# Graph 0's receiver logits on VectorE and the last graph's first row on TensorE, in a four-layer graph-network kernel on one core

## The chip, the cores and the metric

The kernel runs on one core of a Trainium2 chip. The metric is the device time of one execution in microseconds (us). Three runs of the kernel before took 2438.94, 2440.05 and 2445.26 us, so the median is 2440.05. An execution with a profile took 2434.94 us; what the profile shows of it is a span of 2433.1 us.

A matrix product in float32 appears in the trace as two records, each with a weight load of its own. A transpose appears as one.

## The reference, cut to what matters

There are 16 graphs of 1024 nodes with 256 features, and a dense integer adjacency for each. Four layers follow one another; each begins with a layer norm and a ReLU and ends with a residual sum.

```python
# layer 0: attention, softmax over axis 1
h = jnp.matmul(input, W)
f1 = jnp.einsum('bnf,f->bn', h, a1)          # the receiver's logit
f2 = jnp.einsum('bnf,f->bn', h, a2)
e = leaky_relu(f1[:, :, None] + f2[:, None, :], 0.2)
attention = softmax(jnp.where(adj > 0, e, NEG_BIG), axis=1)
out = elu(attention @ h)
# layer 1: the same with softmax over axis -1
# layer 2: mean of the neighbours' messages, plus an update product and a bias, relu
# layer 3: four heads of 64; attention with slope 0.01, then per head:
out = relu(attention @ h + bias) + h
out = (out - mu) / sqrt(var + 1e-6) * ln_gamma + ln_beta
x = x + out
```

## The kernel before

The graphs are the outer loop. Each graph is a generator, `graph(b)` (L1272), that yields between small steps; the loop at L1319 pulls the generators in the order of due times, so that neighbouring graphs overlap. That order only fixes how the instructions are emitted. At the end `Order(tc, slots).run()` (L1348) lists them anew: it has a price for each instruction and a rank from TensorE's cumulative cost, walks through a model of the engines, and then fixes the order of each engine's queue. Each queue is served strictly in that order, so an instruction that waits holds all behind it.

A layer works on eight tiles of 128 nodes (NT = 8). `Norm.pair` (L854) takes two tiles: statistics, then `shifted` (L896) makes hn, the shifted and rectified tile, on ScalarE; `flip` (L904) transposes it on TensorE and ScalarE copies it into ht. The scale 1/std is not applied there, but at the eviction of the projection: `project` (L916) multiplies ht by the weights wx, to which one or two columns W a are appended, and an eviction on ScalarE (L999, L1061, L1172) multiplies by rs. rs comes from GpSimd (`inv_std`, L822), by a power.

The attention weight is not computed as exp(leaky_relu(f1 + f2)) but from products of exponentials: a tile of p (128 x 1024) is the larger of two terms times the mask (layer 0: L1027 and L1029; layer 1: L1088; layer 3: L1195). For that the receiver's logit must stand as a row on all partitions. There are two ways to get this row:

- `spread` (L925) and `everywhere` (L942): the column is transposed, its exponential is written to memory by a DMA (d_row), and a second DMA spreads it to all partitions (row). All layers with a row use it, apart from the next case.
- the class `Row` (L947): for each tile VectorE multiplies the identity by the logits (diag, L956), and TensorE multiplies a matrix of ones by diag (L957); two PSUM banks hold the row, and ScalarE writes its exponential (L963). Graph 0 uses it in layers 0 and 1.

In layer 0 the logit is column D of the evicted projection hs, so that each diag follows an eviction:

```python
            ps = project(norm, wx[0], n, D + 2)
            nc.scalar.activation(hs[:, n, : D + 2], ps[:, : D + 2], AF.Copy, scale=norm.rs[n])
            if by_pe:
                by_pe.add(n, hs[:, n, D : D + 1])
            m.step()
```

The mask is loaded in 16 raw pieces of 128 x 512 integers through SP's queue into three buffers (`Mask`, L779); `step` (L800) turns a piece into bytes and a sum, on VectorE for graph 0 (L808), on ScalarE for the others (L810), and starts the next load. After each p of layer 0, hs is divided by the sum of p (L1030, L1031), and the products with it go to PSUM. A part of the output tiles ("early", L1014 to L1016) is accumulated while the p's are still being made: four for graph 0, two for the others. The other tiles follow after the last p. For layer 0 each tile then has two evictions on ScalarE (L1049, L1051) and the residual on VectorE (`residual`, L979), which feeds the next norm.

PSUM has eight banks in four pools of two: tr (transposes), mm (projections and the prepared weight columns ps_wa), at and hd (output tiles; hd also for the row of the class `Row`, layer 2's outputs and layer 3's heads).

Some loads must not start too early: `behind` (L713) lets VectorE write one element of the target, copied from the latest p of graph 0, so that the load waits for that p.

In layer 3 (L1164) the four heads take eight p's each from a row per head; the row buffers are two. `tail` (L1220) then normalises each head: reciprocal and product, sum with hs, mean, squares on ScalarE (L1242), sums (L1250), the power on GpSimd, gamma, the scale (L1262), beta (L1264), the residual (L1268) and the output's DMA on SP (L1269). The tail of one graph lies beside the next graph's layers, except for the last graph's.

At the very end a count of conditions is taken (L1329 to L1347, t_bad and bad): were all values in range. It is summed over the partitions by TensorE (L1344) into a flag, which every engine reads (L1359); a general kernel runs if it isn't zero.

## Time and profile before

| What | Value |
|---|---|
| runs | 2438.94, 2440.05, 2445.26 us; median 2440.05 |
| profiled execution | 2434.94 us, span 2433.1 us, mean granted clock 0.991 |
| busy: TensorE, VectorE, ScalarE, GpSimd | 2355.2, 1966.0, 1448.6, 467.2 us |
| graph 0: first p (L1027) begins, last L1029 ends | 29.83, 49.99 us |
| graph 0: first product with a p (L1019) begins | 34.74 us |
| graph 0: first hs of layer 1 (L1061), first product of layer 1 (L1081) | 71.22, 83.34 us |
| last graph: layer 2's products end, first p of layer 3 | 2342.7, 2362.06 us |
| last graph: last p ends, last L1268 begins | 2400.4, 2425.20 us |

A line of the profile's groups or timelines names the line of the kernel, the engine, the operation, the tiles written and read, and the count; times are in microseconds after the start of the span. What stands in brackets is the time that the engine stood idle before and what ended that wait. The chain of waits goes back from the last instruction to what released each step.

### The profile page before, as it was taken

The page shows a single profiled execution, that of the slowest core. Times are in us where ns is not written, and L with a number is a line of the kernel's source. Part 1 is how long each engine was busy: PE and PEld are TensorE (multiplying, and loading weights), DVE is VectorE, ACT ScalarE, POOL GpSimd, SP SyncE. Part 2 cuts the span into 40 slices and gives each one's busy share as a digit, 9 for nine tenths or more (in the row PEclk, how much of TensorE's full clock was granted, in tenths as well). Part 3 has the DMA queues.
Part 4 walks back from the last instruction along what each step waited for, and adds up shares of the span by engine and source line. Part 5 has one row for each costly group of instructions (what it writes and reads, how often), then busy time and mean ns, then how long its engine had stood idle before and what let it go on. Part 6 is the DMA issues. An engine that isn't in the chain of part 4 may idle for free.

```text
span 2433.1 us, 63096 instructions
## 1 busy us (share of the span) xinstructions
PE 2355.2 (97%) x26224; PEld 2102.6 (86%) x26224; DVE 1966.0 (81%) x3862; ACT 1448.6 (60%) x4036; POOL 467.2 (19%) x454
## 2 busy tenths in 40 slices
PE   6999999999999999999999999999999999999974
PEld 5889888988988889888988989888888988989874
DVE  7478697997979889797896979889687897968858
ACT  4665657567475665756567475665757567475440
POOL 1020210303113031220303113031220303112021
PEclk9999999999999999999999999999999999999997
DMA  5452342624344253332624334253342624243031
GB/s 179 86 109 86 73 97 80 143 89 91 94 108 97 84 126 100 77 97 77 142 92 92 93 105 101 84 126 94 82 97 77 142 93 92 93 101 87 19 71 38
DMA packets 212152, 232.17 MB, mean 95 GB/s; under 512 B 10344, under 2 KB 160976, under 8 KB 211856
## 3 DMA queue, kind: packets, MB, share of 16 engines
q0 software_dynamic: 137728, 83.90, 19.2%
q1 hardware_dynamic: 74128, 144.14, 18.3%
q8 instruction: 208, 3.41, 0.6%
q14 instruction: 88, 0.72, 0.1%
HBM read 210.78 MB, written 17.22 MB: 94 GB/s over the span
## 4 chain that ended last, share of the span: by engine, by line
PE 87%; DMA 5%; ACT 3%; DVE 2%; issue 1%; POOL 1%; SPq 0%; POOLq 0%; ACTq 0%; DVEq 0%
PE ps_o L1019 18%; PE ps_o L1208 17%; PE ps_proj L919 17%; PE ps_o L1081 16%; PE ps_o L1149 10%; PE ps_o L1143 5%; DMA raw<-in_adj_t 4%; PE pt_h L913 4%; ACT mask L810 1%; POOL rs L826 0%; DMA d_row<-e_row 0%; ACT hn L900 0%; ACT hi L1135 0%; DMA row<-d_row 0%; DVE p L1088 0%
## 5 line engine op out<-in xcount | busy, mean ns | idle before, releaser
L1195 DVE SCALAR_TENSOR_TENSOR p<-row,q,mask 128x1024 f32<-128x1024 f32 x512 | 617.9, 1280 | 66.7 <-PE ps_o L1208 58.9
L919 PE MATMUL ps_proj<-wx,ht 128*128 128x258 f32 (+2 forms) x2048 | 512.8, 386 | 7.7 <-ACT hs L1172 3.9
L1208 PEld LDWEIGHTS ps_o<-hb,p 128*64 128x64 f32 x16384 | 488.5, 138 | 32.7 <-issue 17.8
L1208 PE MATMUL ps_o<-hb,p 128*64 128x65 f32 x16384 | 502.7, 223 | 9.5 <-DVE p L1195 7.6
L1019 PE MATMUL ps_o<-hs,p 128*128 128x256 f32 x2048 | 477.8, 381 | 8.7 <-ACT hs L1031 8.7
L1081 PE MATMUL ps_o<-hs,p 128*128 128x257 f32 x2048 | 469.0, 382 | 4.1 <-ACT v L1106 2.6
L1081 PEld LDWEIGHTS ps_o<-hs,p 128*128 128x128 f32 x2048 | 381.6, 190 | 61.8 <-ACT v L1106 6.2
L1019 PEld LDWEIGHTS ps_o<-hs,p 128*128 128x128 f32 x2048 | 380.2, 191 | 60.1 <-ACT hs L1031 10.1
L919 PEld LDWEIGHTS ps_proj<-wx,ht 128*128 128x128 f32 x2048 | 371.0, 190 | 68.6 <-ACT hs L999 6.1
L825 POOL TENSOR_SCALAR rs<-mv 128x4 f32<-128x4 f32 (+1 forms) x112 | 44.9, 401 | 1323.6 <-ACT unread L873 1307.2
L826 POOL TENSOR_TENSOR rs<-rs,neg_half 128x4 f32<-128x4 f32 (+2 forms) x144 | 264.0, 1833 | 12.0
L900 ACT ACTIVATE hn<-xs,shift 128x256 f32<-128x256 f32 x384 | 177.2, 503 | 79.8 <-PE pt_h L913 44.9
L1216 ACT ACTIVATE res<-ps_o 128x260 f32<-128x260 f32 x128 | 49.8, 389 | 259.8 <-PE ps_o L1208 259.3
L1149 PE MATMUL ps_o<-hi,adj 128*128 128x258 f32 x1024 | 202.1, 319 | 2.1 <-ACT hi L1135 1.0
L810 ACT ACTIVATE mask<-raw 128x512 uint8<-128x512 int32 x240 | 151.2, 633 | 50.2 <-DMA raw<-in_adj_t 49.5
L913 PE MATMUL pt_h<-ident,hn 128*128 128x128 f32 x1024 | 175.5, 278 | 4.6 <-ACT hn L900 4.3
L989 DVE SCALAR_TENSOR_TENSOR xs<-v,xs 128x256 f32<-128x256 f32 x384 | 160.7, 419 | 17.4 <-ACT v L1106 11.2
L818 POOL DMA_DIRECT2D adj<-in_adj x128 | 114.5, 898 | 293.7 <-PE ps_o L1149 292.0
L1149 PEld LDWEIGHTS ps_o<-hi,adj 128*128 128x128 f32 x1024 | 150.0, 190 | 14.9 <-ACT hi L1135 5.4
L1027 DVE SCALAR_TENSOR_TENSOR p<-row,q 128x1024 f32<-128x1024 f32 x128 | 161.5, 1272 | 1.7 <-DMA row<-d_row 1.4
L913 PEld LDWEIGHTS pt_h<-ident,hn 128*128 128x128 f32 x1024 | 126.7, 141 | 37.1 <-ACT hn L900 7.2
L1088 DVE SCALAR_TENSOR_TENSOR p<-row,q,mask 128x1024 f32<-128x1024 f32 x128 | 155.9, 1273 | 1.4 <-DMA row<-d_row 1.4
(115 smaller groups left out, 2988.1 us busy)
## 6 DMA issues: line engine op xcount, KB each, us to landing
raw<-in_adj_t SPq DMA_DIRECT2D x256, 256.0 KB
adj<-in_adj POOLq DMA_DIRECT2D x128, 512.0 KB, 5.2
row<-d_row SPq DMA_DIRECT2D x109, 512.0 KB
xs<-in_x POOLq DMA_DIRECT2D x32, 512.0 KB, 4.4
out<-xs SPq DMA_DIRECT2D x32, 512.0 KB
wx<-in_w SPq DMA_DIRECT2D x3, 256.0 KB
d_row<-e_row SPq DMA_DIRECT2D x45, 4.0 KB
wts<-in_w_t SPq DMA_DIRECT2D x2, 256.0 KB
```

The costliest lines, as they stand in the source:

```text
L810: nc.scalar.activation(to, raw, AF.Square, accum_out=total)
L826: nc.gpsimd.tensor_tensor(rs[:, :n], rs[:, :n], neg_half[:, :n], op=OP.pow)
L900: nc.scalar.activation(hn, xs[:, 2 * g + k, :], AF.Relu, scale=scale, bias=bias)
L913: nc.tensor.transpose(pt[:, c, k * P : (k + 1) * P], hn[:, c * P : (c + 1) * P], ident)
L919: nc.tensor.matmul(ps[:, :width], norm.ht[:, c, n * P : (n + 1) * P], w[:, c, :width], start=(c == 0), stop=(c == DC - 1))
L989: nc.vector.scalar_tensor_tensor(x, v, 0.0, x, op0=OP.max, op1=OP.add, accum_out=after.sums[:, i % 2 : i % 2 + 1])
L1019: nc.tensor.matmul(ps[:, :D], ps_[j][:, i * P : (i + 1) * P], hs[:, j, :D], start=(j == 0), stop=(j == NT - 1))
L1027: nc.vector.scalar_tensor_tensor(p, row_a, q[:, j : j + 1], row_b, op0=OP.mult, op1=OP.max)
L1081: nc.tensor.matmul(ps[:, : D + 1], ps_[j][:, i * P : (i + 1) * P], hs[:, j, : D + 1], start=(j == 0), stop=(j == NT - 1))
L1149: nc.tensor.matmul(ps[:, : D + 2], adj_n[j][:, i, :], h[:, i, : D + 2], start=False, stop=(h is lo and i == NT - 1), skip_group_check=True,)
L1195: nc.vector.scalar_tensor_tensor(p, row, q[:, jj, h : h + 1], mask[:, jj, :], op0=OP.max, op1=OP.mult)
L1208: nc.tensor.matmul(pss[g][part, k * HW : (k + 1) * HW], ps_[t][:, i * P : (i + 1) * P][:, part], hbv[:, j + t, h, :], start=(j == 0 and t ...
```

## The change

For graph 0's layer 0:

- `weights01` gets, for layer 0 only, one more pair of products: the receiver's weight column W a as a row on all partitions (ps_wr), and a copy of it on ScalarE.
- `shifted` makes, for graph 0's first norm, the logit of each tile directly on VectorE: the sum over hn times that row. After the norm's statistics VectorE multiplies the eight logits by 1/std, and `Row` makes the row before the projections are emitted. q, the sender's exponential, is made tile by tile after each eviction instead of once for all.
- of the 16 mask pieces of graph 0, the eight of the second half (g = 1) are made by ScalarE.
- six output tiles instead of four are accumulated beside the p's; the two added ones use the two banks of mm.

For the last graph:

- the row of the first head in layer 3 comes from `Row` instead of the two DMAs. Those of the heads 1 to 3 still go through memory.
- beta is added to x in layer 3, right after the row, and no longer in the tail.

In the built program the order of TensorE's queue from layer 1 of graph 0 to the end of the last graph's layer 2 is the same as before. In the last graph, the conditions' count stands behind the last p on VectorE, and its flag behind the last L1268 (L1299 there); before, it stood ahead of the first p.

```diff
@@ -740,6 +740,16 @@
                 )
             for k, to in enumerate(order):
                 nc.vector.tensor_copy(t[:, fc, D + to : D + to + 1], ps[:, k : k + 1])
+        if wait:
+            return
+        ps = tile_of(mm_ps, [P, HALF], F32, tag="mm", name="ps_wr", bufs=2)
+        for ec in range(DC):
+            nc.tensor.matmul(
+                ps[:, :D], avs[:, ec, :1].to_broadcast([P, P]), wts[:, ec, :], start=(ec == 0), stop=(ec == DC - 1)
+            )
+        both = tile_of(work, [P, N], F32, tag="p3", name="wr", bufs=5)
+        nc.scalar.copy(both[:, :D], ps[:, :D])
+        rows["receiver"], rows["unread"] = both[:, :D], both[:, D:]
 
     def weights2():
         wx[2] = t = load_w(w2_msg, D, "wx2", 2 * D)
@@ -804,7 +814,7 @@
                 s, n, g, raw = self.raws.pop(0)
                 k = self.b * NT * NHALF + s
                 to, total = self.bytes[:, n, g * HALF : (g + 1) * HALF], squares[:, k : k + 1]
-                if self.b == 0:
+                if self.b == 0 and g == 0:
                     nc.vector.scalar_tensor_tensor(to, raw, 1.0, raw, op0=OP.mult, op1=OP.mult, accum_out=total)
                 else:
                     nc.scalar.activation(to, raw, AF.Square, accum_out=total)
@@ -843,6 +853,7 @@
                 self.scales = tile_of(small, [P, 2, NT], F32, tag="scales", name="scales", bufs=2)
             self.mv = tile_of(small, [P, NT, 2], F32, tag="mv", name="mv", bufs=4)
             self.mean, self.var = self.mv[:, :, 0], self.mv[:, :, 1]
+            self.first = None
 
         def stds(self, n, scale):
 
@@ -899,6 +910,12 @@
                 hn = tile_of(work, [P, D], F32, tag="hn", name="hn", bufs=3)
                 nc.scalar.activation(hn, xs[:, 2 * g + k, :], AF.Relu, scale=scale, bias=bias)
                 hns.append(hn)
+                if self.first is not None:
+                    n = 2 * g + k
+                    nc.vector.scalar_tensor_tensor(
+                        rows["unread"][:, k * D : (k + 1) * D], hn, 1.0, rows["receiver"], op0=OP.mult, op1=OP.mult,
+                        accum_out=self.first[:, n : n + 1],
+                    )
             self.waiting = (g, hns)
 
         def flip(self):
@@ -956,8 +973,8 @@
             nc.vector.tensor_scalar(diag, ident, f, None, op0=OP.mult)
             nc.tensor.matmul(self.ps[g][:, k * P : (k + 1) * P], ones, diag, start=True, stop=True)
 
-        def rows(self, scales):
-            made = [tile_of(work, [P, N], F32, tag="row", name="row", bufs=2) for _ in scales]
+        def rows(self, scales, tag="row"):
+            made = [tile_of(work, [P, N], F32, tag=tag, name="row", bufs=2) for _ in scales]
             for g in range(NHALF):
                 for row, scale in zip(made, scales):
                     nc.scalar.activation(row[:, g * HALF : (g + 1) * HALF], self.ps[g], AF.Exp, scale=scale)
@@ -993,27 +1010,31 @@
 
     def layer0(b, xs, m, norm, after):
         hs = new_hs()
-        by_pe = Row() if b == 0 else None
+        q = tile_of(small, [P, NT], F32, tag="q", name="q", bufs=4)
+        if b == 0:
+            by_pe = Row()
+            nc.vector.tensor_tensor(norm.first, norm.first, norm.power[0], op=OP.mult)
+            for n in range(NT):
+                by_pe.add(n, norm.first[:, n : n + 1])
+            row_a, row_b = by_pe.rows((1.0, S))
         for n in range(NT):
             ps = project(norm, wx[0], n, D + 2)
             nc.scalar.activation(hs[:, n, : D + 2], ps[:, : D + 2], AF.Copy, scale=norm.rs[n])
-            if by_pe:
-                by_pe.add(n, hs[:, n, D : D + 1])
+            if b == 0:
+                nc.scalar.activation(q[:, n : n + 1], hs[:, n, D + 1 : D + 2], AF.Exp, scale=1.0 - S)
             m.step()
             yield 3.85
         mask = m.bytes
-        if by_pe:
-            row_a, row_b = by_pe.rows((1.0, S))
-        else:
+        if b:
             row_a, row_b = [everywhere(d, "row") for d in spread(column(hs[:, :, D : D + 1], 1), 1, (1.0, S), "l0")]
-        q = tile_of(small, [P, NT], F32, tag="q", name="q", bufs=4)
-        nc.scalar.activation(q, hs[:, :, D + 1], AF.Exp, scale=1.0 - S)
+            nc.scalar.activation(q, hs[:, :, D + 1], AF.Exp, scale=1.0 - S)
         watch(b, 0, hs[:, :, D : D + 2])
         yield 5.25
         ps_ = []
         early = [tile_of(at_ps, [P, HALF], F32, tag="at", name="ps_o0", bufs=2) for _ in range(EARLY)]
         if b == 0:
             early += [tile_of(hd_ps, [P, HALF], F32, tag="hd", name="ps_o0", bufs=2) for _ in range(NHALF)]
+            early += [tile_of(mm_ps, [P, HALF], F32, tag="mm", name="ps_o0", bufs=2) for _ in range(2)]
 
         def product(ps, i, j):
                 nc.tensor.matmul(
@@ -1165,11 +1186,14 @@
         hs = new_hs()
         terms = hs[:, :, D:]
         run = 2 if b < B - 1 else 1
+        by_pe = Row() if b == B - 1 else None
         hb = new_hs("hb")
         hbv = hb[:, :, : H * HW].rearrange("p t (h e) -> p t h e", e=HW)
         for n in range(NT):
             ps = project(norm, wx[3], n, W3)
             nc.scalar.activation(hs[:, n, :], ps[:, :W3], AF.Copy, scale=norm.rs[n])
+            if by_pe:
+                by_pe.add(n, terms[:, n, :1])
             if n % 2:
                 pair = slice(n - 1, n + 1)
                 nc.scalar.activation(hbv[:, pair, :, HO], terms[:, pair, H:], AF.Exp, scale=S3)
@@ -1180,7 +1204,13 @@
                 nc.vector.tensor_tensor(t, t, hbv[:, pair, :, HO:].to_broadcast([P, 2, H, HO]), op=OP.mult)
             yield 1.07
         d_row = spread(column(terms[:, :, :H], H), H, (S3 - 1.0,), "l3")
-        row = everywhere(d_row[0], "row3")
+        if by_pe:
+            (row,) = by_pe.rows((S3 - 1.0,), "row3")
+            for g in range(NHALF):
+                part = xs[:, g * PER : (g + 1) * PER, :]
+                nc.vector.tensor_tensor(part, part, rows["beta3"].unsqueeze(1).to_broadcast([P, PER, D]), op=OP.add)
+        else:
+            row = everywhere(d_row[0], "row3")
         watch(b, 2, terms)
         q = tile_of(small, [P, NT, H], F32, tag="q3", name="q3", bufs=2)
         nc.scalar.activation(q, terms[:, :, H:], AF.Exp, scale=1.0 - S3)
@@ -1261,7 +1291,8 @@
                 yield 0.66
             nc.vector.tensor_tensor(o, o, r, op=OP.mult)
             yield 0.00
-            nc.vector.tensor_tensor(of, of, along("beta3"), op=OP.add)
+            if b < B - 1:
+                nc.vector.tensor_tensor(of, of, along("beta3"), op=OP.add)
             yield 5.43
             x = xs[:, t, :]
             xv = x.rearrange("p t (h e) -> p t h e", e=HO)
@@ -1273,6 +1304,8 @@
         xs = loaded.pop(b)
         m = masks.pop(b)
         norm = Norm()
+        if b == 0:
+            norm.first = tile_of(small, [P, NT], F32, tag="q", name="first", bufs=4)
         for g in range(NT // 2):
             norm.pair(xs, g)
             m.step()
```

## The prediction

> **What bounds the kernel now.** First the summary of busy time, then the span in slices: TensorE is busy 97% of the span, and its only weak slices are the first and the last two; its clock is full except in the last.
>
> ```profile
> span 2433.1 us, 63096 instructions
> PE 2355.2 (97%) x26224; PEld 2102.6 (86%) x26224; DVE 1966.0 (81%) x3862; ACT 1448.6 (60%) x4036; POOL 467.2 (19%) x454
> ...
> PE   6999999999999999999999999999999999999974
> DVE  7478697997979889797896979889687897968858
> ...
> PEclk9999999999999999999999999999999999999997
> ```
>
> Next the busy time by stretch (columns: stretch, length, busy us and instructions of PE, its weight loads, DVE, ACT, POOL, then clock, DMA share, GB/s). Between 130 and 2343 us TensorE lacks 11.9 us in all; before 51 us it lacks 20.6, after 2343 us 45.1. All that can be won lies at the two ends.
>
> ```profile
> 30.00:40.00 10.00, 5.26 (x14) 4.02 (x15) 10.00 (x18) 1.52 (x3) 0.00 (x0) 0.66 0.01 3
> ...
> 0.00:51.00 51.00, 30.43 (x128) 24.31 (x128) 37.15 (x121) 19.35 (x44) 5.07 (x11) 0.93 0.50 159
> 130.00:2343.00 2213.00, 2201.15 (x24645) 1972.29 (x24645) 1820.53 (x3525) 1359.15 (x3801) 436.02 (x420) 1.00 0.38 96
> 2343.00:2363.00 20.00, 7.98 (x38) 5.89 (x36) 12.93 (x29) 7.39 (x23) 3.01 (x3) 0.84 0.24 64
> ...
> 2401.00:2433.10 32.10, 0.63 (x22) 0.49 (x18) 21.41 (x20) 2.90 (x4) 9.96 (x4) 0.55 0.11 36
> ```
>
> Then who waited in the first 60 us (us, times, longest), and the timelines of the engines there. TensorE waits for hs scaled by L1031, which waits for VectorE: the first p of graph 0 starts at 29.83, after the row's last exponentials (28.60), and VectorE is 10.00 of 10 us busy from 30 to 50.
>
> ```profile
> PE ps_o L1019 <- ACT hs L1031: 8.7, 3, 6.2
> 28.60 1.09 ACT L963 ACTIVATE row<-ps_row 128x512 f32<-128x512 f32 x2 [0.97 <-PE ps_row L957]
> 29.83 1.28 DVE L1027 SCALAR_TENSOR_TENSOR p<-row,q 128x1024 f32<-128x1024 f32 x1
> 71.22 0.48 ACT L1061 ACTIVATE hs<-ps_proj,rs 128x258 f32<-128x258 f32 x1 [0.28 <-PE ps_proj L919]
> ```
>
> Last the chain of waits near the end (start, us, what) and VectorE's timeline. The final graph's row goes out to memory and back for 6.1 us; then 32 p's run without a gap, 38.35/32 = 1.20 us each; then a tail through POOL's power.
>
> ```profile
> 2355.79 1.38 DMA d_row<-e_row
> 2357.22 4.74 DMA row<-d_row
> ...
> 2418.22 3.43 POOL rs L826
> ...
> 2425.20 1.22 DVE xs L1268
> 2362.06 38.35 DVE L1195 SCALAR_TENSOR_TENSOR p<-row,q,mask 128x1024 f32<-128x1024 f32 x32 [5.26 <-DMA row<-d_row]
> ```
>
> **What the Trainium skill says.** "TensorE: Matmul & The Clock Gate", section "What's actually happening": the array runs at half rate until it has been busy some 3.4 us. The trace agrees in kind: 14 records from 30 to 40 us took 5.26 us, 0.38 each at clock 0.66, against 0.217 later. So the first products after a gap stay dear. "ScalarE: Activation LUTs", section "What ACT_TABLE_LOAD costs": an ACTIVATE has a fixed part of 186 ns, and neighbours overlap by 93; the trace's 128x8 exponential (L1010) takes 0.21, so I price each one-column q at 0.12. "SBUF — State Buffer", section "SBUF: two separate sides": VectorE with two inputs and GpSimd exclude each other; the 128x16 power took 2.90 to 3.87 us in this trace, which fits without proving it. "DMA: Bandwidth & Descriptors", section "Latency and other measured facts": a register load from memory costs about 600 ns; here POOL's flag load shows 0.49.
>
> **The middle.** The instructions of both programs stand in the same order on every engine from layer 1 of graph 0 to the end of the final graph's layer 2 (L1264's two per graph, and q, are the same there). What is won at the start is therefore carried through.
>
> **The start, part by part.**
> Weights: two products L747 (128x256, 0.43 each) and one copy (0.36 as L1051) on TensorE and ScalarE near 10 us. They sit in a gap (TensorE idles 4.1 us before 12.35), but ScalarE now does its table load (1.28) and one mask ahead of the first hn at 11.69: cover about zero, cost 0 to 0.5; I take 0.1.
> Masks: eight of 16 move. VectorE sheds 8 x 0.69 = 5.5; ScalarE gains 8 x 0.72 = 5.8. Two stand ahead of the last four hn, so hn 4 starts at about 16.6 instead of 15.3; the last hn ends at about 18.5 as before (there it had waited 1.85 for a transpose). The order of SP's loads is unchanged, but a raw buffer is now free when ScalarE is done: raw 3 is done at about 15.9 instead of 13.7, so raw 6 (3.0 after issue) comes at about 18.9 and VectorE waits for it with three logits behind.
> Logits: eight L915 of 128x256, priced as L989 (0.35 + 0.08) = 3.4 on VectorE. They end at about 20.6; eight diagonals at 0.2 and a mask end at 23.0.
> ScalarE then sets the date: from 18.5 it runs two ht (0.47), six hs (0.40), five q (0.12), two masks (0.72) and four row halves (0.50), 0.94 + 2.4 + 0.6 + 1.44 + 2.0 = 7.4, and about 0.4 of waits for projections that stand behind ps_row in TensorE's queue. The row is whole at 26.3, so the first p starts **3.5 earlier**. (If ScalarE's share weighed nothing, VectorE would let it start at 24.0; if raws come late, 28.)
> p's: before, 29.83 to 50.0 = 20.2. One mask (0.69) and L974 (0.13) join it, four weight copies (0.3) leave: 20.7, end at 47.0; the scaled hs of the last one at about 48.7, since four masks of graph 1 queue ahead of it.
> Six tiles: each p now feeds 6 products of 0.433 = 2.6, about what VectorE needs per p (2.5), so TensorE stays busy: first product at 31.0, the first 12 records cold (4.5 instead of 2.6), the last p's products 51.3 to 53.9. Two tiles stay behind instead of four. From 48.7: 28 products x 0.433 = 12.1, the four ps_wa of layer 1, which now wait for an mm bank, 0.95, twelve transposes x 0.11 = 1.3: 63.1, against 70.1. ScalarE meanwhile has 12 evictions, six hn, six squares and three ht back to back and is free at 63.2: it is as late as TensorE. The first hs of layer 1 then starts at 64.6 against 71.22, 6.6 earlier; one mask (0.72) stands after it that was not there. **Start: -6.0.** Bounds: -2 (raws or ScalarE late) and -9 (row at 24.0 and no mask in the way).
>
> **The end, part by part.**
> Row: out goes the wait from 2355.2 to 2362.06. VectorE is now the path: from 2345.4 it has eight diagonals x 0.2 = 1.6, eight hb passes x 0.61 = 4.9, L1264, L1268 and one added L1211 at 1.14 = 3.4, and 0.3 of small ones: 10.2, so the first p at 2355.7; I take 2355.9. By the other way round: last hs about 2353.8, diagonal, ps_row 0.22, row half 0.5: 2355.4, hidden. The first beta pass fits the 1.16 idle before 2339.46 and costs nothing; without that it costs 1.14. **-6.2.** Head 1's row still goes through memory: column 2355.2, plus 0.6, 1.4 and 4.7 = 2362; needed eight p's later, 2365.5, so 3 us of slack. SP's queue loses one 512 KB row; graph 14's two outputs stay behind head 1's row.
> Tail: L1264 leaves twice (1.14 each) and the first L1268 moves into the wait for POOL: -2.3. But the check that had filled VectorE's gap now runs in the tail: four instructions in the 1.21 wait for L1216 are free, three (0.6) fall on the path, and the first L1250 now stands behind the second L1239 (1.14): POOL starts 1.75 later. Sum **-0.5**, bounds -2.3 and +1.5.
> The flag is ready only after the last L1268. Its load (about 0.6) runs beside the last output, 6.7 us from L1268 to the end of the span: 0, up to +1 if it is not covered. The first output no longer overlaps the second: 0 to -0.7, taken as **-0.3**.
>
> **Sum.** -6.0 - 6.2 - 0.5 - 0.3 = -13.0. Span 2433.1 to 2420.1; the profiled execution's own time 2434.9 to 2421.9. The runs' median is 2440.05, 5.1 above the profiled one; the same saving gives **2427.0**.
>
> **Rivals.** (1) The cover is shallow: ScalarE, late at 26 and again at 63, hands the six tiles' gain back, start -2, end -5: **2433**. For it: ScalarE has no gap in my count between 52 and 64. Against: ScalarE waited 3.9 there before. This is also how the change would fail to do what it says. (2) All goes well: start -9, end -9: **2422**. For it: VectorE alone would allow 24.0; against: the order of ScalarE's queue. (3) Slower: the three raw buffers, freed by two engines in turn, bring the loads into single file. At 3.46 from issue to landing (raw 5 before, 12.99 to 16.45) plus 0.7, 16 in series last 67 us, the last mask comes at about 76 and the p's end 27 later than before; minus 7 at the end: **2460**. It is slower once the last p passes 57; in the trace three loads fly together, which speaks against it.
>
> **Chances.** Forecast 0.60, with 2423.5 to 2431 of its own; (1) 0.21; (2) 0.15; (3) 0.04. The range 2420 to 2434.5 leaves out (3) and the outer edges of (1) and (2). A measurement of this kernel can tell about 0.3% from no change, 7.3 us, which is 2432.7: all of the forecast and (2) and under half of (1) lie beyond: faster 0.83, same 0.13, slower 0.04.
>
> **What would show it.** First p of graph 0 near 26; the wait L1019 for L1031 down from 8.7 to about 3; first L1061 hs near 64.6; first L1195 of the final graph some 13.2 us after layer 2's last product instead of 19.4 (2342.7 to 2362.1); 32 p's still 38.3; POOL's first power of the tail some 14 us after the last p's end instead of 12.2 (2400.4 to 2412.6). Wrong if the first p is after 28, if layer 1 starts after 69, or if the output's end follows the flag.

## The result and the profile after

The changed kernel takes 2429.33 us (median of 6 runs, 2428.39 to 2430.09), the kernel before 2439.9 us (6 runs beside them, 2436.2 to 2445.91): ratio 0.9962, 95% interval 0.995 to 0.9974. The forecast was 2427.0. In a later session the same two kernels gave 2429.33 (15 runs) against 2437.03 (26 runs), ratio 0.9968 [0.9957, 0.9978]; the medians lie 10.6 and 7.7 us apart, the two intervals together reach from 5.4 to 12.2 us, and the forecast 13.0 lies outside both.

The profiled execution took 2429.41 us, its span is 2428.0; that is only 5.1 less than the span of before. A single pair of profiles is a poor witness here: spans of unchanged code differ by several us from one execution to the next (first experiment). The accounts below therefore use marks that are read from several profiles each.

From the page of the changed kernel, the busy time and the slices of TensorE, VectorE and TensorE's clock:

```profile
span 2428.0 us, 63180 instructions
PE 2361.5 (97%) x26244; PEld 2106.7 (87%) x26244; DVE 1964.4 (81%) x3871; ACT 1455.2 (60%) x4062; POOL 469.3 (19%) x454
...
PE   7999999999999999999999999999999999999984
...
DVE  6478697996979888787897969879787896978867
...
PEclk9999999999999999999999999999999999999997
```

TensorE gained a tenth in the first slice and one in the slice before the last, VectorE lost one in the first. By stretch (columns as before), the first 51 us now hold 35.72 us of TensorE's work instead of 30.43, and the middle is as it was, 10.8 us of idle time against 11.9:

```profile
0.00:51.00 51.00, 35.72 (x142) 27.91 (x143) 34.87 (x120) 24.66 (x67) 5.37 (x11) 0.93 0.49 155
30.00:40.00 10.00, 5.90 (x15) 4.77 (x16) 10.00 (x21) 2.95 (x11) 0.00 (x0) 0.66 0.18 54
130.00:2343.00 2213.00, 2202.22 (x24643) 1972.46 (x24642) 1822.94 (x3527) 1359.47 (x3800) 438.37 (x420) 1.00 0.40 96
```

The waits of the first 60 us (us, times, longest). TensorE's wait for the scaled hs fell from 8.7 to 4.3 (about 3 was expected), and new ones stand around the row: for the weights' product, and for an adjacency load:

```profile
PE ps_o L1040 <- ACT hs L1052: 4.3, 1, 4.3
...
DVE mask L818 <- DMA raw<-in_adj_t: 2.1, 2, 1.3
...
DVE p L1048 <- ACT row L980: 1.6, 1, 1.6
...
ACT wr L751 <- PE ps_wr L747: 1.3, 1, 1.3
```

The timelines of the start, TensorE, ScalarE and VectorE (start, us, engine and line):

```profile
10.46 2.04 PE L747 MATMUL ps_wr<-wts,avs 128*128 128x256 f32 x4 [1.06 <-DVE wx L742]
...
12.54 0.37 ACT L751 COPY wr<-ps_wr 128x256 f32<-128x256 f32 x1 [1.32 <-PE ps_wr L747]
12.81 0.91 ACT L911 ACTIVATE hn<-xs,shift 128x256 f32<-128x256 f32 x2
...
16.92 0.59 ACT L931 COPY ht<-pt_h 128x512 f32<-128x512 f32 x1 [1.34 <-PE pt_h L930]
17.41 0.63 ACT L820 ACTIVATE mask<-raw 128x512 uint8<-128x512 int32 x1
...
18.64 1.70 ACT L911 ACTIVATE hn<-xs,shift 128x256 f32<-128x256 f32 x4
...
20.89 0.69 DVE L818 SCALAR_TENSOR_TENSOR mask<-raw 128x512 uint8<-128x512 int32 x1 [1.28 <-DMA raw<-in_adj_t]
...
25.12 0.48 ACT L1022 ACTIVATE hs<-ps_proj,rs 128x258 f32<-128x258 f32 x1 [1.70 <-PE ps_proj L936]
...
28.48 0.60 ACT L980 ACTIVATE row<-ps_row 128x512 f32<-128x512 f32 x1
...
29.11 1.28 DVE L1048 SCALAR_TENSOR_TENSOR p<-row,q 128x1024 f32<-128x1024 f32 x1 [1.56 <-ACT row L980]
```

The first p of graph 0 starts at 29.11, not at the forecast 26.3: the last hn ends at 20.3 instead of 18.5, and from there to the row's last half ScalarE needs 8.7 instead of 7.8.

The same view at the end (GpSimd, VectorE, TensorE):

```profile
2346.05 3.26 POOL L836 TENSOR_TENSOR rs<-rs,neg_half 128x4 f32<-128x4 f32 x1
...
2347.77 0.68 DVE L1204 TENSOR_TENSOR hb<-hb 128x512 f32<-128x512 f32 x1
...
2349.88 2.60 PE L936 MATMUL ps_proj<-wx,ht 128*128 128x264 f32 x6 [3.23 <-ACT hs L1194]
...
2356.23 38.35 DVE L1225 SCALAR_TENSOR_TENSOR p<-row,q,mask 128x1024 f32<-128x1024 f32 x32
```

The wait for the row's transfer is gone, and the 32 p's take 38.35 us as before. But the power ahead of the last graph's scales now takes 3.26 us (1.33 before), ScalarE and TensorE wait for it, and the six records of projections behind that wait take 2.60 us.

| mean over profiles, us | old part | changed part | difference | forecast |
|---|---|---|---|---|
| first hn of graph 0 | 11.90 | 13.02 | +1.1 | +0.1 |
| first p of graph 0 | 29.95 | 29.66 | -0.3 | -3.5 |
| first p to the last z (p's) | 20.23 | 20.66 | +0.4 | +0.5 |
| last z to layer 1's first hs | 21.12 | 18.00 | -3.1 | -3.6 |
| that hs to layer 1's first product | 12.12 | 12.43 | +0.3 | +0.7 |
| last graph: first projection to layer 3's first p | 20.94 | 17.04 | -3.9 | -6.2 |
| that p to the last residual sum's end | 64.36 | 62.54 | -1.8 | -0.5 |
| from there to the end of the span | 6.93 | 9.22 | +2.3 | -0.3 |
| sum without the first row | | | -6.1 | -13.0 |

A z is the sum of a p, and its mark is the start of the last reciprocal (L1051). The start's means are over 3 profiles of the old start (the kernel before twice, and the one with the end alone) and 7 of the changed one; the end's over 3 of the old end (the kernel before twice, and the one with the start alone) and 6 of the changed one. The measured interval of the second session, -5.4 to -10.5 us, holds the sum.

The first row needs care. VectorE's first statistics, which stand behind the first mask piece and so behind its load, began at 9.91 to 10.71 us in the old start and at 10.02 to 10.98 in the changed one, on the mean 0.3 later. From there to the first hn it is 1.69 to 1.70 us in the three old profiles and 2.51 to 2.52 in the seven changed ones. So 0.8 of the 1.1 belongs to the change, and 0.3 to loads that came later. The seven first p's lie between 28.78 and 31.41, so that the 0.3 of the second row is less than what one execution differs from another.

### The profile page after: what moved, and what is told of

The parts are those of the page before. It is cut to its first block, busy times and chain, and to the rows that moved or that the text cites. A ratio compares the mean times of both kernels' runs of the same rounds, so it can differ in the third digit from the quotient of the medians.

```text
span 2428.0 us, 63180 instructions
## 1 busy us (share of the span) xinstructions
PE 2361.5 (97%) x26244; PEld 2106.7 (87%) x26244; DVE 1964.4 (81%) x3871; ACT 1455.2 (60%) x4062; POOL 469.3 (19%) x454
## 3 DMA queue, kind: packets, MB, share of 16 engines
q1 hardware_dynamic: 73984, 143.62, 18.9%
## 4 chain that ended last, share of the span: by engine, by line
PE 86%; DMA 5%; ACT 4%; DVE 3%; POOL 1%; issue 1%; SPq 0%; ACTq 0%; DVEq 0%
PE ps_o L1238 18%; PE ps_o L1040 17%; PE ps_proj L936 17%; PE ps_o L1102 16%; PE ps_o L1170 10%; PE ps_o L1164 4%; PE pt_h L930 4%; DMA raw<-in_adj_t 4%; ACT mask L820 1%; DVE p L1225 1%; POOL rs L836 1%; ACT hn L911 1%; ACT hi L1156 1%; DMA d_row<-e_row 0%; DMA row<-d_row 0%
## 5 line engine op out<-in xcount | busy, mean ns | idle before, releaser
L1225 DVE SCALAR_TENSOR_TENSOR p<-row,q,mask 128x1024 f32<-128x1024 f32 x512 | 617.9, 1279 | 63.0 <-PE ps_o L1238 58.6
L820 ACT ACTIVATE mask<-raw 128x512 uint8<-128x512 int32 x248 | 156.1, 632 | 53.6 <-DMA raw<-in_adj_t 52.7
L931 ACT COPY ht<-pt_h 128x512 f32<-128x512 f32 x256 | 147.1, 575 | 16.8 <-PE pt_h L930 14.0
```

What stands on the lines that cost most here:

```text
L820: nc.scalar.activation(to, raw, AF.Square, accum_out=total)
L1225: nc.vector.scalar_tensor_tensor(p, row, q[:, jj, h : h + 1], mask[:, jj, :], op0=OP.max, op1=OP.mult)
```

## The experiments

**The parts, and the spread.** The kernel before and the changed kernel once more, and each half of the change alone.

Kernel before, unchanged: 

> The kernel before, unchanged, once more. Its six runs lay between 2436.2 and 2445.9 us, its profiled execution at 2434.9; the changed kernel's six runs lay between 2428.4 and 2430.1. Theory A (the spread of the kernel before is chance of its loads, in no one place): ratio 1.000 within 0.3%, runs again spread over some 5 to 10 us, and a profile that differs from the first at the start (first p of graph 0 between 28 and 33). Rival B (the first profile was typical and the other runs had a disturbance from outside): the runs now lie within 2 us at about 2435.

Measured: 2435.8 us against 2436.75 for the same kernel beside it (56 runs), ratio 0.9995 [0.9985, 1.0006]; those 56 runs reach from 2430.75 to 2445.3, and this profile's span is 2436.7 against 2433.1. The runs are not within 2 us, so a single disturbance from outside is not the explanation; where the spread arises is open. From layer 1's first product to the last graph's first projection, code that no kernel here changes, the profiles take 2256.0 to 2261.6.

The start alone:

```
-        by_pe = Row() if b == B - 1 else None
+        by_pe = None
...
-            if b < B - 1:
-                nc.vector.tensor_tensor(of, of, along("beta3"), op=OP.add)
+            nc.vector.tensor_tensor(of, of, along("beta3"), op=OP.add)
```

> The start's parts of the change alone: logits on VectorE, masks divided, six tiles; the last graph as before. By the two profiles the start is worth 2.8 us at the first product of layer 1 (80.53 against 83.34) and 3.5 at the end of the last graph's layer 2 (2339.0 against 2342.5). Theory A: -3 to -4 against the profile of before (span about 2429.5), and if the spread of the kernel before comes from its start, the runs become as close together as those of the changed kernel, at about 2431. Rival B, the start is worth nearly all that was measured (10.6): about 2429.5 in the runs. Rival C, the spread comes from the last graph: runs still 5 to 10 us apart, median near 2436.

The end alone, the kernel before with the layer3 and tail hunks and the tag of Row.rows: 

> The last graph's parts alone: first row by TensorE, beta first; graph 0 as before. Theory A: the row gives 2.3 us, the tail 1.8, and the flag, now behind the last sum, costs 2.5 after it: -1.6 against the profile of before (span about 2431.5). Span from the last sum of the residual to the end about 9 us, as in the changed kernel, instead of 6.7. Rival C, the spread of the kernel before comes from its last graph's row through memory: the runs close up here and the median falls by 5 or more.

Both, again: 

> The changed kernel, unchanged, once more, so that the parts can be compared in one session. The start alone gave 2435.3 us and the end alone 2433.6, against 2436.75 before: -1.4 and -3.1. Theory A (the parts add up, and the first measurement of the kernel before lay high): about -5 to -7, 2430 to 2432. Rival B (the parts together give more than their sum): -9 to -10 as first measured, about 2427.

| kernel | median, us (runs) | ratio to before, 95% |
|---|---|---|
| start alone | 2435.32 (21) | 0.9993 [0.9985, 1.0] |
| end alone | 2433.62 (22) | 0.9987 [0.998, 0.9995] |
| both, second session | 2429.33 (15) | 0.9968 [0.9957, 0.9978] |

The start is worth 0 to 3.7 us, the end 1.2 to 4.9, both together 5.4 to 10.5. The start's -6.0 is ruled out; that the parts add up is within the intervals, and no more can be said.

**The flag.** The count of conditions ahead of and beside the first p's of the last graph, as before the change, all else as changed. The two functions hold the lines of the count, moved from the end of the program:

```
+        if b == B - 1:
+            checked = check_most()
         d_row = spread(column(terms[:, :, :H], H), H, (S3 - 1.0,), "l3")
...
         watch(b, 2, terms)
+        if b == B - 1:
+            check_top(*checked)
```

> The changed kernel, with the conditions' count emitted before and beside the last graph's first p's, so that the flag is there before the tail. Theory A, every engine reads the flag and branches only after the last sum and that is exposed (9.2 us from the last L1299 to the end of the span, 6.7 before): -2.5 at the end, -0.6 to -1.7 in the tail, +1.5 beside the p's: 1.5 to 2.5 us below the changed kernel, and 6.5 to 7 us from last sum to the end. Rival D, the longer end is the output's transfer itself: the 9.2 stay and the kernel is 0 to 1 us slower than the changed one.

Measured: 2429.52 us (10 runs), 0.9964 [0.9952, 0.9976]; the medians don't separate it from the changed kernel. The profile does: from the end of the last residual sum to the end of the span 6.5 us, against 9.3. The records of the branch line show why (queue, event, its ns, when). First the changed kernel, then this one:

```profile
L1393 PEldq COMPARE_BRANCH  x1: 4584/4584/4584, 2419.5 to 2419.5; - x1
```

```profile
L1402 PEldq COMPARE_BRANCH  x1: 3684/3684/3684, 2399.3 to 2399.3; - x1
```

In these two profiles TensorE's queue needs 4.6 and 3.7 us for the branch on the flag, where VectorE's needs 0.076. With the flag set early this lies beside the tail; in the changed kernel it starts at 2419.5, 0.6 us after the flag, and SyncE's closing events begin only after its end at 2424.0. What the tail had saved (1.8) is handed back. Part of it returns in this kernel as the count's own work: first p to last residual sum 63.23 us, not 62.54.

**Where the start's gain comes from.** Four tiles beside the p's, as before, all else changed:

```
-            early += [tile_of(mm_ps, [P, HALF], F32, tag="mm", name="ps_o0", bufs=2) for _ in range(2)]
```

> The changed kernel with four tiles beside the p's instead of six. The first p came only 0.7 us earlier and the p's ended only 0.3 earlier, yet layer 1 began 2.8 us earlier. Theory A, the six tiles alone bring that: two tiles of 8 products at 0.433 = 6.9 us come back behind the last p, of which ScalarE's queue had hidden some 3: +2.5 to +3.5 over the changed kernel, and the first product of layer 1 back near 83.5. Rival B, the gain comes from the earlier logits: 0 to +1.

Measured: 2430.11 us (9 runs), 0.9967 [0.9954, 0.998], which the runs cannot tell from the changed kernel; last z to layer 1's first hs 19.3 us in the one profile, against 18.0 with six tiles (17.3 to 18.7 in seven profiles) and 21.1 before. So the two tiles are worth some 1.3, and 1.8 come without them: my theory of 2.5 to 3.5 for the tiles fell. Not all of the 1.8 is a gain, since the p's took 21.0 us here and 20.2 before: counted from the first p to layer 1's first product it is 53.5 before, 52.5 with four tiles and 51.1 with six. TensorE's timeline of the kernel before, of this one and of the changed one, in this order, tells where the 1.8 come from:

```profile
46.15 3.72 PE L1019 MATMUL ps_o<-hs,p 128*128 128x256 f32 x16 [1.31 <-ACT hs L1031]
51.08 6.63 PE L1019 MATMUL ps_o<-hs,p 128*128 128x256 f32 x28 [1.21 <-ACT hs L1031]
```

```profile
45.79 10.22 PE L1039 MATMUL ps_o<-hs,p 128*128 128x256 f32 x44
```

```profile
41.82 17.21 PE L1040 MATMUL ps_o<-hs,p 128*128 128x256 f32 x79
```

Before, TensorE stood twice for a scaled hs, 2.5 us in all: ScalarE scaled these hs in pairs, at 45.60 and 50.53, behind masks of graph 1 that waited for their loads (2.98 us ahead of the first pair, 0.56 and 0.90 ahead of the second). With four tiles in the changed order each of them leaves alone, as soon as VectorE's z is there, and TensorE runs through. With six it runs through as well, from 41.82. This is read from one trace of each; ScalarE's order by itself was not tried, so that it is the cause is likely and not shown.

**What held the first p.** The product for the receiver's weights in PSUM banks of another pool:

```
-        ps = tile_of(mm_ps, [P, HALF], F32, tag="mm", name="ps_wr", bufs=2)
+        ps = tile_of(at_ps, [P, HALF], F32, tag="at", name="ps_wr", bufs=2)
```

> The changed kernel with the receiver's weight row (ps_wr) in a bank of the at pool instead of mm. In the changed kernel ps_wr waited 1.06 us for VectorE's copy to free an mm bank and its own copy stood ahead of the first hn, which came at 12.81 instead of 11.69. Theory A: ps_wr follows the weight columns at once, the first hn comes back to about 11.8, and the first p comes 0.5 to 1 us earlier (28.1 to 28.6); total 0.3 to 1 us less. Rival B, the row's date is set by the raw pieces (the mask on VectorE at 20.89 with three logits behind it), so first p and total stay within 0.3 us.

Measured: 2427.59 us (6 runs), 0.9952 [0.9934, 0.997], which overlaps the changed kernel's interval; first hn at 12.45, first p at 28.61. Taken as dates both are earlier by about what one execution differs from another. Counted from VectorE's first statistics they are clearer:

```profile
10.48 0.42 DVE L875 BATCH_NORM_STATS2 st<-xs 128x6 f32<-128x256 f32 x1
...
12.45 0.90 ACT L911 ACTIVATE hn<-xs,shift 128x256 f32<-128x256 f32 x2
```

The first hn comes 1.97 us after the statistics, against 2.51 to 2.52 in seven profiles with the old bank and 1.69 to 1.70 before the change. The first p comes 18.1 us after them, against 18.7 to 19.1 in six of the seven (20.8 in the seventh), and layer 1's first product at 79.04, against 80.75 on the mean. So the wait for the bank cost about 0.55 of the 0.8 us at the first hn, and in this one profile that reached the first p.

All of graph 0's masks on VectorE:

```
-                if self.b == 0 and g == 0:
+                if self.b == 0:
```

> The changed kernel with all of graph 0's masks on VectorE, as before the change (the logits by VectorE, the six tiles and the final row stay). Theory A (at the start ScalarE's queue sets hn, and so hs and the row; VectorE has room): the last hn comes 1.2 us earlier, at about 19 instead of 20.2 us, the first p 0.5 to 1.5 us earlier, at 27.7 to 28.7; but three masks of 0.65 us more fall between the p's, so that the p phase is 1.5 to 2 us longer and layer 1 starts 0.5 to 1 us later: 2430. Theory B (VectorE's queue is what bounds the row): its four extra masks before the first p push the first p to 30 or later, and layer 1 by 2 to 3 us: 2432.

Measured: 2429.47 us (6 runs), 0.9967 [0.9955, 0.998]. The timelines of ScalarE and VectorE:

```profile
19.84 0.51 ACT L911 ACTIVATE hn<-xs,shift 128x256 f32<-128x256 f32 x1
...
26.50 0.69 DVE L818 SCALAR_TENSOR_TENSOR mask<-raw 128x512 uint8<-128x512 int32 x1 [0.70 <-DMA raw<-in_adj_t]
...
27.11 1.28 DVE L1048 SCALAR_TENSOR_TENSOR p<-row,q 128x1024 f32<-128x1024 f32 x1
```

The last hn ends as late as with the masks on ScalarE (20.35), so that part of the theory fell. But from there to the whole row it is 6.5 us instead of 8.7: no masks stand between, and the wait of 1.70 for a projection is gone. The first p comes at 27.11, ahead of the expected band and 2.0 before the changed kernel's profile, though 0.9 of this is an earlier load of the first mask piece in this execution (VectorE's first statistics at 9.44 and not 10.30). The p's then take 21.9 instead of 20.7, and layer 1's first product comes at 78.5 against 80.75 on the mean (79.2 to 82.5). With the earlier load taken off, some 1.2 us are left there, within that spread. So the masks on ScalarE delay the first p; that layer 1 starts later for them is not shown, and the runs don't show it either.

**The last graph's row.** beta3 back in the tail, the row still by TensorE:

```
-            for g in range(NHALF):
-                part = xs[:, g * PER : (g + 1) * PER, :]
-                nc.vector.tensor_tensor(part, part, rows["beta3"].unsqueeze(1).to_broadcast([P, PER, D]), op=OP.add)
...
-            if b < B - 1:
-                nc.vector.tensor_tensor(of, of, along("beta3"), op=OP.add)
+            nc.vector.tensor_tensor(of, of, along("beta3"), op=OP.add)
```

> The changed kernel with beta back in the tail of the last graph; the row stays with TensorE. In the changed kernel GpSimd's power of 128x4 took 3.26 us (in three profiles) instead of 1.33 and 1.01 of before, and layer 3's last four evictions wait for it. Theory A, VectorE's added pass L1211 with its two inputs lies beside this power and holds it up: the power takes 1.0 to 2.0 here, the first p of layer 3 comes 1.3 to 2 us earlier, and the tail is longer by 1.1 to 2.3: within 1 us of the changed kernel. Rival B, the power is long because of the hb passes that are moved there as well: still 3 us or more, no earlier first p, and the kernel is 1 to 2 us slower than the changed one.

Measured: 2428.49 us (9 runs), 0.9963 [0.995, 0.9976]. The power still took 3.26 us, so that theory A fell: other passes of VectorE had moved into the place of beta's. The stretch to layer 3's first p is nevertheless 14.73 us, against 15.59 in the second profile of the changed kernel, whose projections ran as fast; so beta's pass itself cost 0.9 there. The end of the span came 6.9 us after the last residual sum: the flag is now set before that sum ends, and the branch runs beside it.

Then the same with VectorE emptied at that place, by making the two passes over hb for the first six tiles at once, behind the sixth:

```
-            if n % 2:
+            if n % 2 and (b < B - 1 or n > 3):
                 pair = slice(n - 1, n + 1)
+                if b == B - 1 and n == 5:
+                    pair = slice(0, 6)
...
```

> The changed kernel with beta3 back in the last tail, and with VectorE's two passes over hb of the last graph's first six tiles made in one go behind the sixth (instead of pair by pair). VectorE then has only the two last passes of the seventh graph's tail between the normalisation's sums and the wait for GpSimd's power, and they end at about the power's start. Theory A (the power of 128x4 is locked out while VectorE's passes over two SBUF inputs follow each other, and ends 0.9 us after the last of them): the power takes 1.0 to 1.6 us instead of 3.26, hs starts about 2 us earlier; the six tiles' passes then come late, so that the first p gains 0 to 1 us only. Theory B (a power at this place costs 3.26 whatever VectorE does): 3.26 again, and the first p is 2 us later than in the changed kernel. Time: A 2428.5, B 2431.

Measured: 2426.12 us (5 runs, 2425.2 to 2427.85), 0.9959 [0.9945, 0.9972]; the interval overlaps the changed kernel's. Its timelines of VectorE, GpSimd and TensorE:

```profile
2344.69 0.28 DVE L973 TENSOR_SCALAR diag<-ident,hs 128x128 f32<-128x128 f32 x1
2344.91 1.01 POOL L836 TENSOR_TENSOR rs<-rs,neg_half 128x4 f32<-128x4 f32 x1
2346.79 0.71 PE L936 MATMUL ps_proj<-wx,ht 128*128 128x264 f32 x2 [1.06 <-ACT hs L1194]
...
2352.49 6.07 DVE L1225 SCALAR_TENSOR_TENSOR p<-row,q,mask 128x1024 f32<-128x1024 f32 x5
```

The power takes 1.01 us here, where VectorE has no two-input pass beside it. In the changed kernel it began within 0.03 us of the first of three such passes that follow each other without a gap, and ended 0.86 us after the third (2348.45 to 2349.31 in the lines of its profile above); the eight other profiles with 3.26 us show the same, at 0.86 to 0.87. So VectorE's passes hold it up. The Trainium skill says in "SBUF — State Buffer", section "SBUF: two separate sides", that a VectorE operation with two SBUF inputs and a GpSimd operation that reads SBUF exclude each other for the whole instruction. The trace agrees in kind. How many passes the power has to sit out is not always the same, as the kernel before shows in an earlier graph:

```profile
588.13 1.28 DVE L1027 SCALAR_TENSOR_TENSOR p<-row,q 128x1024 f32<-128x1024 f32 x1
588.34 1.96 POOL L826 TENSOR_TENSOR rs<-rs,neg_half 128x4 f32<-128x4 f32 x1
589.33 0.42 DVE L1159 TENSOR_TENSOR v<-v,row_bias 128x256 f32<-128x256 f32 x1
```

This power began inside a pass and ended 0.89 us after that pass (589.41 to 590.30), although the next one followed at once; 16 powers of that trace took 1.95 or 1.96 us in this way. Passes that began after the power, be it only 0.03 or 0.17 us after it, did not lengthen it (1.01 to 1.03 us). Why three passes had to end first in the last graph stays open.

From the first projection to the first p it is now 13.60 us (against 17.0 on the mean in the changed kernel, and 14.73 with the power still at 3.26).

TensorE kept busy in the wait for the power, with beta3 where the change has it (the products are extra, nothing reads them):

```
             ps = project(norm, wx[3], n, W3)
+            if by_pe and n == 5:
+                spare = tile_of(tr_ps, [P, P], F32, tag="tr", name="ps_spare", bufs=2)
+                for _ in range(12):
+                    nc.tensor.matmul(spare, ones, ident, start=True, stop=True)
```

> The changed kernel with twelve extra products of ones and the identity (128x128, into a spare PSUM tile that nothing reads) on TensorE in the last graph, after the fourth row piece, where it otherwise waits some 3.2 us for hs. Theory A (TensorE's clock falls after that wait, in some executions, and the two projections behind it then take twice as long): the wait is filled, the six records of projections that followed it take 1.6 us and not 2.6, and the stretch from the last graph's first projection to layer 3's first p is 15.6 us or less; the median falls by 0.5 to 1 us below the changed kernel's, to about 2428.5, since about half of the executions had the low clock. Theory B (the clock there follows something else than this gap): the extra products run at half speed themselves in some executions (0.5 us a product and not 0.25), the projections behind them start 1 to 3 us later, and the stretch is 17 to 19 us.

Measured: 2426.62 us (5 runs, 2426.12 to 2428.8), 0.9959 [0.9945, 0.9972]. Its timeline of TensorE:

```profile
2348.16 2.40 PE L1197 MATMUL ps_spare<-ident,ones 128*128 128x128 f32 x20
2351.14 1.60 PE L936 MATMUL ps_proj<-wx,ht 128*128 128x264 f32 x6 [0.59 <-ACT hs L1198]
```

The projections take 1.60 us and the stretch 15.59, as theory A has it. Over all profiles: behind a wait of 3.2 to 3.7 us the projections ran at about half speed in 7 of 11 (2.60 to 3.01 us for six records, 3.70 and 3.89 for eight) and at full speed in 4 (1.60 for six, 2.05 for eight, this one in the first profile of before). Behind a wait of 0.6 to 1.1 us (this kernel, the previous one and the next) they ran at full speed in 3 of 3. The granted clock settles what the half speed is. Here are these projections in the two profiles of the changed kernel; the clock stands third from the end:

```profile
2349.88:2352.48 2.60, 2.60 (x7) 2.06 (x8) 2.52 (x5) 1.01 (x3) 0.00 (x0) 0.59 0.00 0
```

```profile
2347.05:2348.65 1.60, 1.60 (x8) 1.41 (x9) 1.52 (x4) 0.94 (x3) 0.00 (x0) 1.00 0.00 0
```

In all seven slow cases it was 0.50 to 0.59 during the projections, in the seven fast ones 1.00. So a gap of this length let the clock fall in some executions; three are too few to prove that the shorter gap saves it always. The runs cannot separate this kernel from the changed one, whose interval overlaps.

**What the runs point to.** The kernel with beta3 in the tail and the late passes over hb, with all of graph 0's masks on VectorE and the weights' product in the other bank as well: 

> The last experiment's good parts in one kernel: the changed kernel with beta3 in the last tail and hb of the last graph's first six tiles in one go (power 1.01 us there), all of graph 0's masks on VectorE (first p at 27.1 in one profile), and the product for the receiver's row in a PSUM bank of its own. Theory A (the three act at different places and add up): the stretch from the last graph's first projection to layer 3's first p is 13.6 us, the flag stays hidden (7.1 us from the last residual sum to the end), layer 1's first product comes at 78 to 80; the median is 2424.5, some 2 us below that of the kernel with the first part alone and 4.5 below the changed kernel's. Theory B (at the start the later masks give back what the first p gains, and the bank changes nothing): the median is 2426 to 2427, that of the first part alone.

Measured: 2421.17 us (5 runs, 2419.34 to 2422.19) against 2432.98 for the kernel before beside it (9 runs), ratio 0.9945 [0.9931, 0.9958]. The marks are those of its parts: first p at 27.33, layer 1's first product at 79.17, 13.61 us to layer 3's first p, 6.5 from the last residual sum to the end. The ratio is the lowest of all kernels. Its median is the only one below 2425, but the kernel before, run beside it, was some 4 us faster as well than in the second session. Its interval still overlaps that of the kernel with beta3 in the tail and the late hb passes alone (0.9945 to 0.9972), so that the start's share in it, theory A's 2 us, is not shown by the runs. In the profile layer 1's first product is no earlier than with the other bank alone (79.04): the masks on VectorE give back in the p's, 22.1 us, what the first p gained, as theory B has it.

## Why the prediction was right, and where it was not

The direction and the size of the whole held: measured -10.6 in the session of the forecast and -7.7 later, against -13.0. The steps held less well, and that the number came within 2.3 us is in part luck: the 2440.05 that the forecast started from lies 3.3 above the median of the 56 later runs, and the marks add up to -6.1 where -13.0 was forecast. Of the three signs of being wrong two came: the first p is after 28 (28.8 to 31.4), and the end of the span follows the flag. Layer 1's first hs, at 68.3 on the mean (66.8 to 70.1), kept within its limit of 69, but far from the 64.6 of the forecast.

*The start, -6.0.* It was -2.7. The p's (+0.5) and what lies behind them (-3.6) came out at +0.4 and -3.1, although I had credited the six tiles with all of it, and the profile gives them 1.3; the rest came, it seems, from ScalarE's order, which I had not priced. The step that failed is the date of the row: "The row is whole at 26.3, so the first p starts **3.5 earlier**". It was 0.3 earlier. One reading was wrong and two terms were mis-sized. Its "the last hn ends at about 18.5 as before" takes a start for an end: in the kernel before the last hn begins at 18.47 and ends at 18.98. The weights' product was priced at "0 to 0.5; I take 0.1": its four records took 2.04 us, about 0.43 us apart where later ones stand 0.217 apart, and began only when VectorE's weight copy had freed a bank; its copy is the first thing in front of the first hn, which the change makes 0.8 us later. ScalarE's "0.4 of waits for projections" were 1.70. The two masks behind the last hn were priced, but with all masks on VectorE they and that wait are gone, and the first p came at 27.1 (0.9 of it by an earlier load). The third case of that bracket, late loads and 28, was seen as well: the load of raw 6 came at 20.9 and not at 18.9, and VectorE waited 1.28 us for it, yet the row waited for ScalarE.

*The final row, -6.2.* It was -3.9. "VectorE is now the path", 10.2 us of its work, left out that GpSimd's power can wait until VectorE's passes end. I had named the exclusion of the two engines and seen it in the 128x16 powers, and did not apply it to the 128x4 power that the scales of the last four tiles hang on. Where TensorE's clock stayed high the stretch was 15.59, 2.4 later than my 13.2, and the power's 3.26 instead of 1.01 us is 2.25 of that. The 13.60 with the lock out of the way is not my term come true, since beta's pass, 1.14 in the term, is gone there as well. The other part is TensorE's clock behind the 3.2 us wait, up to 2.2 us in one execution, which the first profile of before happened not to show.

*The tail, -0.5.* It was -1.8: the two beta passes and their place gave -2.3 as forecast (with the count early, 23.7 us from the last p's end to the last residual sum's end, against 26.0 before), the count on the path +1.3 instead of +1.75, and the first power took 2.90 instead of 3.75 us.

*The flag, "0, up to +1", and the output, -0.3.* Together they were +2.3, the one step with the wrong sign. I had taken the flag's load for its cost and overlooked the branch behind it, which holds TensorE's queue for 3.5 to 4.6 us and in the kernel before ran at 2401.5, 24 us ahead of the last residual sum.

*The rivals.* Rival (1) gave -2 at the start and -5 at the end; its -7 is nearer than -13.0 to the -6.1 of the marks and to the -7.7 of the later session, and only the first session, with its high base, puts the forecast nearer. Its mechanism is right in part: ScalarE was late at 26, and in the profile of the changed kernel it has no gap from 55.6 to layer 1's first hs at 68.1. TensorE has none there either, so that ScalarE taking back the six tiles' gain is not shown. Rival (3) did not occur: the raw loads came later by 2 us, not in single file.

## What to carry to other kernels

A wait that is filled with VectorE passes is not free if GpSimd has something on the path there: look for two-input passes that run when its instruction starts, and end them before. When a last flag or a branch is moved to the end of a program, price what every queue does behind it, not only the load. And where one engine's date decides, sum its queue with the waits for engines that are cold or ordered behind new work: these, not the instructions' own durations, were the larger error here.

## What the runs showed of the hardware that was not expected

- The branch on a loaded value took 3.5 to 4.6 us on TensorE's queue in all 14 profiles, 0.045 to 0.076 on the others. Why is open.
- A 128x4 power on GpSimd took 1.01 us alone and 3.26 where it began together with a run of three two-input passes of VectorE, ending 0.86 to 0.87 after the last of them; inside a single pass it ended 0.89 after that pass, though another followed (1.96), and with a pass that began after it, from 0.03 us on, it took 1.01 to 1.03.
- After a wait of 3.2 to 3.7 us TensorE ran at about half speed in 7 of 11 profiles (granted clock 0.50 to 0.59) and at full speed in 4 (1.00), with the same instructions: 2.60 to 3.01 or 1.60 us for six records. The Trainium skill, "TensorE: Matmul & The Clock Gate", section "What's actually happening", says that the array runs at half rate until it has been busy for some 3.4 us, that it falls back after an idle window of about that length, and that these windows run free of the kernel. A gap of about one window, met at a different point of it in each execution, would give both outcomes; no run here tests that.
